# A graph attention kernel: when and where the gathers of source rows are issued

## The chip, the cores and the metric

The kernel runs on one core of a Trainium2 chip. The metric is device time in microseconds, the median of the runs shown. Five engines work side by side, each through its own list of instructions in order: PE (matmul), DVE (vector), ACT (scalar), POOL (GpSimd) and SP, which here only issues DMAs. They wait for one another by semaphores. POOL issues the indirect DMAs, which fetch table rows by a list of indices.

## The reference

One relational graph attention layer on 3125 nodes of 128 features and 100000 edges sorted by destination, with 5 edge types and 8 heads of 16 features, and two layer norms behind it. Cut to what matters:

```python
for r in range(R):
    q = einsum('eh,khd->ekd', x[dst], W_Q[r]); k = einsum('eh,khd->ekd', x[src], W_K[r])
    v = einsum('eh,khd->ekd', x[src], W_V[r])
    logits = (q * k).sum(-1) / 4 + attn_bias[r]            # only edges of type r
    e = exp(logits - segment_max(logits, dst)[dst])
    out += segment_sum(e / (segment_sum(e, dst)[dst] + 1e-12) * v, dst)
out = out.reshape(n, 128) @ out_proj_w.T + out_proj_b
h = layernorm(out + x) * ln_gamma + ln_beta
return layernorm(x + h)
```

## The kernel before

A first phase multiplies all nodes with all key and value weights and stores the rows in a table in HBM, `kv_d` (one row of 256 floats for each node and type), and the first queries in `q_d`. When the table is complete, the edges are worked through in 196 groups of 512 edges; a group is 4 tiles of 128 edges (`T = 4`).

The loop (L1062) counts steps `k`. In step k the logits of group k are made, and the values of an older group v are weighed with its softmax weights: weighing needs each destination node's maximum, and that needs the logits of all its edges. The distance is 16 to 18 steps at the start and 19 from group 22 on. All engines' orders are the order in which this loop emits instructions. What bears on the change:

- `gather(g)` (L678) fetches the key and value rows of group g into buffer `kvs_[g % KVB]`, 128 rows for each of 4 indirect DMAs, 1 KB a row, on POOL. The indices are columns of `idx`. A buffer may be written again when `weigh` (L878) of the group that was in it is done. There are `KVB = 22` buffers.
- `KVA = 9` groups are gathered ahead of the loop (L1059). In the loop, step k emits the gather of group k+2 (`AHEAD = 2`; k+1 in the last 16 steps), before the step's weighing (L1085).
- `logits(g)` (L756) multiplies the gathered keys with the spread queries on DVE and sums by head; `store_logits` (L764) writes them to `lg_d` from SP's queue.
- `maxima_load(b)` (L770) is an indirect DMA too, on POOL: it fetches for each of 128 nodes of block b the logits of its up to 64 edges (`ell`). It is emitted one step after the last group that may hold an edge of the block, behind this step's gathers. `maxima` (L779) works on it on ACT and DVE in the three following steps, 3, 4 and 5 of eight.
- The order on DVE within a step: `residual`, `weigh`, `less_max` of the next group to be weighed, `norm`, `logits`, `spot` (the 0/1 matrix `hot`, L735), the queries' remainders, `maxima`, `norms`. On PE: `spread_m`, `sums`, `spread_q`. On SP: the fetches of three steps ahead, stores of finished blocks, `fetch_m`, and the logits' store.

The lines of the loop that the change touches:

```python
        while gathered < NGR - 1 and step_of[gathered + 1] <= k + (AHEAD if k < final - 16 else 1):
            gathered += 1
            gather(gathered)
        for b in range(NM):
            if full_step[b] + 1 == k:
                maxima_load(b)
```

Of the kernel before, what the change touches and what calls it, by code (L numbers as in the profile page):

```python
# [10 lines left out]
I32 = mybir.dt.int32  # L11
# [6 lines left out]
P = 128  # L18
# [22 lines left out]
T = GE // P  # L41
NGR = -(-E // GE)
# [11 lines left out]
AHEAD = 2  # L54
# [5 lines left out]
SB = P * E // N // SR  # L60
SPAD = 5
QB = 3
KVB = 22
HELD = 21
KVA = 9


@with_exitstack
# [40 lines left out]
def full_at(n, more=0):  # L109

    last = E // N * n + slack(n) + more
    return -(-min(E, last) // GE) - 1 if n < N else NGR - 1


def block_of(g, ends=tuple(P * (b + 1) for b in range(NT))):

    return min(
        b for b, n in enumerate(ends)
        if n >= N or E // N * n - slack(n) >= min(E, (g + 1) * GE)
    )  # L120
# [9 lines left out]
NM = len(MB)  # L130


def windowed_path(
# [4 lines left out]
    nc = tc.nc  # L138
# [4 lines left out]
    kv_d = dram.tile([((NT - 1) * P + 64) * R, KVW], F32, name="kv_d")  # L143
# [6 lines left out]
    def keep(name, shape, dt=F32):  # L150
        return const.tile(shape, dt, name=name)

    idx = keep("idx", [P, T, NGR], I32)
# [19 lines left out]
    def buffers(those):  # L173
        for i in those:
            kvs_[i] = ctx.enter_context(tc.tile_pool(name=f"kvp{i}", bufs=1)).tile(
                [P, T, KVW], F32, name=f"kv{i}"
            )

    at_once = range(KVA)
    buffers(at_once)  # L180
# [184 lines left out]
    def fetch_keys(g):  # L365
        kt = ahead.tile([P, T, P], BF16, name="kt")
        nc.sync.dma_start(kt.rearrange("w t p -> w (t p)"), key_d[g].partition_broadcast(P))
        live["kt", g] = kt

    def fetch_q(g):  # L370
        qw = ahead.tile([P, 3, H], BF16, name="qw")
        f = window(g, first5, SPE)
        nc.sync.dma_start(qw.rearrange("w s h -> w (s h)"), q_d[bass.ds(f, P), :])
        live["qw", g] = qw
# [268 lines left out]
    rows, counted = {}, 0  # L643
# [29 lines left out]
    ps = ctx.enter_context(tc.tile_pool(name="ps", bufs=2, space=PSUM))  # L673
    buffers(i for i in range(KVB) if i not in at_once)
    hold = ctx.enter_context(tc.tile_pool(name="hold", bufs=HELD))
    flow = ctx.enter_context(tc.tile_pool(name="flow", bufs=2))
    late_flow = ctx.enter_context(tc.tile_pool(name="late_flow", bufs=2))
    def gather(g):  # L678
        kv = kvs_[g % KVB]
        for t in range(T):  # L680
            nc.gpsimd.indirect_dma_start(  # L681
                out=kv[:, t, :], out_offset=None, in_=kv_d[:, :],
                in_offset=bass.IndirectOffsetOnAxis(ap=idx[:, t, g : g + 1], axis=0),
            )


    def fetch_x(name, b):
# [68 lines left out]
    def logits(g):  # L756
        kv, lg = kvs_[g % KVB], live["lg", g]
        prod = flow.tile([P, T, H], F32, name="prod", bufs=1)
        nc.vector.tensor_tensor(prod, kv[:, :, :H], live.pop(("qe", g)), op=ALU.mult)  # L759
        nc.vector.tensor_reduce(  # L760
            lg[:, :, :HEADS], prod.rearrange("p t (k d) -> p t k d", d=HD), AX.X, ALU.add
        )

    def store_logits(g):  # L764
        nc.sync.dma_start(
            lg_d[g * GE : (g + 1) * GE, :].rearrange("(p t) c -> p (t c)", t=T),
            live["lg", g].rearrange("p t c -> p (t c)"),
        )

    def maxima_load(b):  # L770
        ell = late_flow.tile([P, D, LW], F32, name="ell", bufs=1)
        nc.gpsimd.indirect_dma_start(  # L772
            out=ell.rearrange("p s c -> p (s c)"), out_offset=None,
            in_=lg_d[: (full_at(MEND[b], D) + 1) * GE, :],
            in_offset=bass.IndirectOffsetOnAxis(ap=start_i[:, b : b + 1], axis=0),
        )
        live["ell", b] = ell
# [100 lines left out]
    def weigh(g):  # L878
        wv, kv = late_flow.tile([P, T, PW], F32, name="wv"), kvs_[g % KVB]
        live["wv", g] = wv  # L880
        nc.vector.tensor_tensor(  # L881
            wv[:, :, :H].rearrange("p t (k d) -> p t k d", d=HD),
            kv[:, :, H:].rearrange("p t (k d) -> p t k d", d=HD),
            live["mde", g][:, :, :, None].to_broadcast([P, T, HEADS, HD]),
            op=ALU.mult,
        )
# [60 lines left out]
    def by_node(g):  # L947
        f = window(g, first, ACTE)
        nc.scalar.copy(oT[:, bass.ds(f, WN)], live.pop(("op", g)))  # L949
# [63 lines left out]
    def store_z(b):  # L1013
        n = min(P, N - b * P)
        nc.sync.dma_start(out[b * P : b * P + n, :], live.pop(("z", b))[:n, :])


    step_of, n = {}, 0
# [4 lines left out]
    final = step_of[NGR - 1]  # L1023
# [5 lines left out]
    full_step = [step_of[full_at(n, D)] for n in MEND]  # L1029
# [3 lines left out]
    at_k, k = {}, 0  # L1033
    for v in range(NGR):
        k = max(k + 1, ready[block_of(v, MEND)])
# [21 lines left out]

    gathered = 0
    for gathered in range(KVA):  # L1059
        gather(gathered)  # L1060
    assert all(q_from[b] >= 2 for b in range(QB, NT))
    for k in range(-2, root_at[NT] + 2):  # L1062
        v, g = v_at.get(k), group_at.get(k)
        q_step = {k - f: b for b, f in enumerate(q_from) if b >= QB and -2 <= k - f <= 5}

        if k >= 0 and k + 3 in group_at:
            fetch_keys(group_at[k + 3])
            fetch_q(group_at[k + 3])
        if -2 in q_step:
            fetch_x("xq", q_step[-2])  # L1070
        for b in range(NT):
            if done_at[b] - 1 == k:
                fetch_x("xr", b)
            if norm_at[b + 1] + 1 == k:
                store_z(b)
        for b in range(NM):
            if ready[b] - 3 == k:
                store_m(b)
        if 5 in q_step:
            store_q(q_step[5])  # L1080
        for u in range(NGR):
            if max(at_k[u] - 3, ready[block_of(u, MEND)] - 2) == k:
                fetch_m(u)

        while gathered < NGR - 1 and step_of[gathered + 1] <= k + (AHEAD if k < final - 16 else 1):  # L1085
            gathered += 1
            gather(gathered)
        for b in range(NM):
            if full_step[b] + 1 == k:
                maxima_load(b)  # L1090

        for b in range(NT):
            if done_at[b] + 1 == k:
                residual(b)
        if v_at.get(k - 4) is not None:
            by_node(v_at[k - 4])
        if v_at.get(k - 2) is not None:
            carry(v_at[k - 2])
        if 1 in q_step:
            turned(q_step[1])  # L1100
        if 3 in q_step or 4 in q_step:
            second_part()
        if 2 in q_step or 3 in q_step:
            first_part()

        if v_at.get(k + 1) is not None:
            spread_m(v_at[k + 1], 8 if k + 1 in group_at else 12)
        if v_at.get(k - 1) is not None or v_at.get(k - 3) is not None:
            sums(v_at.get(k - 1), v_at.get(k - 3))
        if k + 1 in group_at:  # L1110
            spread_q(group_at[k + 1])

        if v is not None:
            weigh(v)
        if v_at.get(k + 1) is not None:
            less_max(v_at[k + 1])
            exps(v_at[k + 1])
        if v is not None:
            weights(v)
        if k + 1 in group_at:  # L1120
            types(group_at[k + 1])
        if v_at.get(k - 2) is not None:
            norm(v_at[k - 2])
        if g is not None:
            logits(g)
            store_logits(g)
        if k + 2 in group_at:
            spot(group_at[k + 2])
        if v_at.get(k + 1) is not None:
            places(v_at[k + 1], 2 if k >= final - 1 else 0)  # L1130
        if 3 in q_step or 4 in q_step:
            third_part()
        if 2 in q_step or 3 in q_step:
            remainder()
        for b in range(NM):
            whole = MB[b][2] is None
            if ready[b] - 6 == k and whole:
                maxima(b, 0, 2)
            if ready[b] - 5 == k and whole:
                maxima(b, 2, 4)  # L1140
            if ready[b] - 4 == k:
                maxima(b, 4 if whole else 0, R)
        for b in range(NT):
            if done_at[b] == k:
                project(b)
        for b in range(NT + 1):
            if root_at[b] == k:
                roots(b)
            if norm_at[b] == k:
                norms(b)  # L1150
        if 0 in q_step:
            turn_q(q_step[0])
        if 1 in q_step:
            queries(q_step[1], 0, RH)
        if 2 in q_step:
            queries(q_step[2], RH, R)
# [505 lines left out]
```

## Time and profile before

| | us |
|---|---|
| timed runs, median (range of 3) | 1240.98 (1237.96 to 1241.49) |
| profiled execution, its own time | 1596.71 |
| its span in the profile | 1594.9 |
| first gather issued, last one issued | 89.1, 1516.8 |
| busy: PE, DVE, ACT, POOL | 978.5, 931.1, 636.1, 797.2 |
| mean granted PE clock | 0.707 of full speed |

The profiled execution is longer than the timed runs by 356 us; durations of single instructions come from it. Some groups of instructions of the page's list, each with line, engine, operation, written and read tiles, count, busy time and mean ns of one, and the idle time of the engine just before them with what ended it:

```profile
L759 DVE TENSOR_TENSOR prod<-kv,qe 128x512 f32<-128x512 f32 x196 | 132.8, 678 | 83.2 <-remote 62.1
L881 DVE TENSOR_TENSOR wv<-kv,me 128x512 f32<-128x512 f32 x196 | 132.8, 677 | 42.1 <-remote 32.6
...
L772 POOL DMA_INDIRECT ell<-lg_d,start_i x25 | 23.6, 945 | 149.1 <-DMA lg_d<-lg 52.4
```

"remote" is a wait whose releaser the profile does not tell; "issue" is time in which the engine waited for nothing that the profile shows. [...]

### The profile page before, as it was taken

How to read it: one execution, taken by the hardware profiler on the slowest of the kernel's cores; microseconds unless marked ns; L12 is line 12 of the kernel's file. 1: busy time of each engine (PE TensorE's matmuls, PEld its weight loads, DVE VectorE, ACT ScalarE, POOL GpSimd, SP SyncE). 2: the span in 40 equal slices, each digit the busy share in tenths (PEclk: the TensorE clock that was granted, in tenths of full speed). 3: DMA queues.
4: the chain of work that ended last, by engine and by line, in shares of the span. 5: the costliest groups of instructions: out<-in, count | busy, mean ns of one | idle time of the engine just before them, and what ended most of it. 6: DMA issues, size and time to landing. Idle time of an engine off the chain costs nothing. (4 is left out here: it accounts for less than half of the span.)

```text
span 1594.9 us, 25686 instructions
## 1 busy us (share of the span) xinstructions
PE 978.5 (61%) x7526; PEld 752.9 (47%) x7526; DVE 931.1 (58%) x2559; ACT 636.1 (40%) x2248; POOL 797.2 (50%) x901
## 2 busy tenths in 40 slices
PE   7931423655676676667566657566676556565786
PEld 3520322434555554555454545455555444454664
DVE  5521623645756656656655656556665665664786
ACT  2620121324434444443453444343444344344454
POOL 3455446254555555555555555555555555455400
PEclk9965556766777767777776777676777777767678
DMA  6963634444545545555554554455555455444410
GB/s 191 357 195 97 153 85 128 103 109 122 139 120 128 144 121 121 138 131 122 119 132 105 133 136 121 117 133 123 129 138 133 111 138 134 111 127 119 102 27 15
DMA packets 180889, 203.63 MB, mean 128 GB/s; under 512 B 83207, under 2 KB 146083, under 8 KB 180620
## 3 DMA queue, kind: packets, MB, share of 16 engines
q0 software_dynamic: 40896, 113.39, 25.4%
q1 hardware_dynamic: 135414, 83.80, 23.4%
q10 hardware_dynamic: 4430, 4.71, 1.2%
q8 instruction: 63, 1.03, 0.3%
q14 instruction: 86, 0.70, 0.2%
HBM read 166.50 MB, written 35.28 MB: 127 GB/s over the span
## 5 line engine op out<-in xcount | busy, mean ns | idle before, releaser
L681 POOL DMA_INDIRECT kv<-kv_d,idx x784 | 742.5, 947 | 534.3 <-DVE den L936 252.9
L915 PE MATMUL pp<-wv,at 128*125 128x136 f32 x1568 | 399.6, 386 | 68.3 <-issue 62.1
L915 PEld LDWEIGHTS pp<-wv,at 128*125 128x125 f32 x1568 | 298.1, 256 | 154.8 <-issue 149.9
L746 PE MATMUL qe<-qw,hot 125*128 125x128 bf16 x2352 | 235.3, 261 | 139.9 <-issue 69.1
L863 PE MATMUL me<-mw,hot 125*128 125x64 bf16 (+1 forms) x2352 | 150.4, 217 | 237.5 <-issue 112.2
L746 PEld LDWEIGHTS <-hot 125*128 125x128 bf16 x2352 | 207.9, 127 | 158.4 <-issue 89.0
L872 DVE TENSOR_TENSOR me<-lg,me 128x32 f32<-128x32 f32 x196 | 37.8, 193 | 395.8 <-remote 247.0
L863 PEld LDWEIGHTS <-hot 125*128 125x128 bf16 x2352 | 130.9, 114 | 264.6 <-issue 232.9
L876 ACT ACTIVATE me<-me 128x32 f32<-128x32 f32 x196 | 35.7, 182 | 511.7 <-DVE me L872 318.6
L901 ACT ACTIVATE at<-row_at,nkey 128x125 f32<-128x125 f32 x744 | 237.5, 398 | 0.0
L759 DVE TENSOR_TENSOR prod<-kv,qe 128x512 f32<-128x512 f32 x196 | 132.8, 678 | 83.2 <-remote 62.1
L881 DVE TENSOR_TENSOR wv<-kv,me 128x512 f32<-128x512 f32 x196 | 132.8, 677 | 42.1 <-remote 32.6
L760 DVE TENSOR_REDUCE lg<-prod 128x32 f32<-128x512 f32 x196 | 134.4, 686 | 6.7
L904 ACT ACTIVATE at<-at 128x500 f32<-128x500 f32 (+1 forms) x196 | 117.4, 599 | 6.2
L917 PE MATMUL pp<-pt,carried 125*5 125x136 f32 x390 | 100.4, 346 | 30.7 <-issue 16.3
L707 PE MATMUL prq<-wq,xTq 128*128 128x384 f32 (+1 forms) x88 | 48.5, 639 | 81.0 <-DVE rem L717 59.9
L772 POOL DMA_INDIRECT ell<-lg_d,start_i x25 | 23.6, 945 | 149.1 <-DMA lg_d<-lg 52.4
L924 PEld LDWEIGHTS pp<-rsum,o 125*128 125x128 f32 x392 | 84.0, 258 | 18.7 <-issue 18.1
L949 ACT COPY oT<-pp 128x25 f32 x196 | 33.7, 172 | 135.9 <-remote 89.1
L810 DVE TENSOR_TENSOR wl<-by_head,shut 128x1024 f32<-128x1024 f32 (+2 forms) x73 | 76.9, 1053 | 17.2 <-issue 10.3
L924 PE MATMUL pp<-rsum,o 125*128 125x25 f32 x392 | 74.4, 270 | 18.3 <-issue 13.7
L816 DVE TENSOR_REDUCE mx<-wl 128x16 f32<-128x1024 f32 (+2 forms) x73 | 76.5, 1048 | 2.5
(184 smaller groups left out, 1018.6 us busy)
## 6 DMA issues: line engine op xcount, KB each, us to landing
kt<-key_d SPq DMA_DIRECT2D x196, 128.0 KB
qw<-q_d SPq DMA_DIRECT2D x196, 96.0 KB
kv_d<-kvs SPq DMA_DIRECT2D x24, 640.0 KB
kv<-kv_d,idx POOLq DMA_INDIRECT x784
q_d<-q SPq DMA_DIRECT2D x22, 480.0 KB
lg_d<-lg SPq DMA_DIRECT2D x196, 18.0 KB
mw<-m_d SPq DMA_DIRECT2D x196, 6.0 KB
xr<-in_x SPq DMA_DIRECT2D x24, 64.0 KB
```

Of the source, the lines that this page charges most:

```text
L681: nc.gpsimd.indirect_dma_start(out=kv[:, t, :], out_offset=None, in_=kv_d[:, :], in_offset=bass.IndirectOffsetOnAxis(ap=idx[:, t, g : g + ...
L746: nc.tensor.matmul(qe[:, t, :], hot[:, t, :], qw[:WR, s, :], start=(s == 0), stop=(s == 2))
L759: nc.vector.tensor_tensor(prod, kv[:, :, :H], live.pop(("qe", g)), op=ALU.mult)
L760: nc.vector.tensor_reduce(lg[:, :, :HEADS], prod.rearrange("p t (k d) -> p t k d", d=HD), AX.X, ALU.add)
L810: nc.vector.tensor_tensor(wl, by_head[:, None].to_broadcast([P, n, nh, D]), shut[:, :n, None, :].to_broadcast([P, n, nh, D]), op=ALU.add,)
L863: nc.tensor.matmul(me[:, t], hot[:, t, :], mw[:WR, None, :, s, :].to_broadcast([WR, times, 2, HEADS // 2]), start=(s == 0), stop=(s == 2),)
L881: nc.vector.tensor_tensor(wv[:, :, :H].rearrange("p t (k d) -> p t k d", d=HD), kv[:, :, H:].rearrange("p t (k d) -> p t k d", d=HD), live ...
L901: nc.scalar.activation(at[:, t, :], row_at[:, :WR], AF.Abs, bias=nkey[:, t, g : g + 1], scale=1.0)
L904: nc.scalar.activation(at[:, on_dve:], at[:, on_dve:], AF.Relu, bias=1.0, scale=-1.0)
L915: nc.tensor.matmul(pp, at[:, t, :], wv[:, t, :], start=(t == 0), stop=(t == T - 1))
L917: nc.tensor.matmul(pp[:R], carried[:WR, g, :], live.pop(("pt", g - 1)), start=False, stop=False,)
L924: nc.tensor.matmul(op, live.pop(("o5", done)), rsum[:WR], start=True, stop=True)
```

## The change

Gathers are issued in two halves. Ahead of the loop 6 groups are gathered instead of 9. In step k the first half (2 tiles) of group k+2 is emitted after this step's weighing. The second half takes its indices from a new small tile, `rows`, which DVE copies from `idx` after this step's logits. The maxima load moves behind the second half. The gathers stay two steps ahead to the end. There are 21 buffers instead of 22.

```diff
-KVB = 22
+KVB = 21
-KVA = 9
+KVA = 6
...
-    def gather(g):
+    def gather(g, t0, rows):
         kv = kvs_[g % KVB]
-        for t in range(T):
+        for t in range(T // 2):
             nc.gpsimd.indirect_dma_start(
-                out=kv[:, t, :], out_offset=None, in_=kv_d[:, :],
-                in_offset=bass.IndirectOffsetOnAxis(ap=idx[:, t, g : g + 1], axis=0),
-            )
+                out=kv[:, t0 + t, :], out_offset=None, in_=kv_d[:, :],
+                in_offset=bass.IndirectOffsetOnAxis(ap=rows(t), axis=0),
+            )
+
+    def first_gathers(g):
+        gather(g, 0, lambda t: idx[:, t, g : g + 1])
+
+    def more_gathers(g):
+        rows = flow.tile([P, T // 2], I32, name="rows", bufs=3)
+        nc.vector.tensor_copy(rows, idx[:, T // 2 :, g])
+        gather(g, T // 2, lambda t: rows[:, t : t + 1])
...
     for gathered in range(KVA):
-        gather(gathered)
+        first_gathers(gathered)
+        gather(gathered, T // 2, lambda t: idx[:, T // 2 + t, gathered : gathered + 1])
...
-        while gathered < NGR - 1 and step_of[gathered + 1] <= k + (AHEAD if k < final - 16 else 1):
-            gathered += 1
-            gather(gathered)
-        for b in range(NM):
-            if full_step[b] + 1 == k:
-                maxima_load(b)
...
         if v is not None:
             weigh(v)
+        ahead_of = []
+        while gathered < NGR - 1 and step_of[gathered + 1] <= k + AHEAD:
+            gathered += 1
+            ahead_of.append(gathered)
+            first_gathers(gathered)
...
         if g is not None:
             logits(g)
             store_logits(g)
+        for u in ahead_of:
+            more_gathers(u)
+        for b in range(NM):
+            if full_step[b] + 1 == k:
+                maxima_load(b)
```

## The prediction

> **What bounds the kernel now.** I read the page's slices first, then the gathers' own row, then the timeline of the loop's start, then a table of stretches, one for each step.
>
> ```profile
> DVE  5521623645756656656655656556665665664786
> ...
> POOL 3455446254555555555555555555555555455400
> ...
> L681 POOL DMA_INDIRECT kv<-kv_d,idx x784 | 742.5, 947 | 534.3 <-DVE den L936 252.9
> ```
>
> By the page no engine is full: DVE is at six tenths, POOL at five, and POOL idles 534 us before its gathers, half of it until the DVE instruction after a weighing. Read alone, this says that compute is late and gathers wait. The loop's start on DVE says why:
>
> ```profile
> 101.06 0.81 DVE L737 TENSOR_SCALAR hot<-kt,row_of 125x512 bf16<-125x512 bf16 x2 [0.64 <-DMA kv<-kv_d,idx]
> 122.19 0.69 DVE L759 TENSOR_TENSOR prod<-kv,qe 128x512 f32<-128x512 f32 x1 [20.31 <-issue]
> 122.91 0.69 DVE L760 TENSOR_REDUCE lg<-prod 128x32 f32<-128x512 f32 x1
> 123.52 0.34 DVE L737 TENSOR_SCALAR hot<-kt,row_of 125x512 bf16<-125x512 bf16 x1
> 154.32 0.69 DVE L759 TENSOR_TENSOR prod<-kv,qe 128x512 f32<-128x512 f32 x1 [30.46 <-remote]
> ```
>
> DVE stands still for 20 and 30 us, and no engine's work ends either wait. What covers both is POOL: it issues 48 gathers without a break from 89.1 to 149.0. In the loop it is the same in small. These are three neighbouring steps, each from one weighing to the next (columns: length, then busy time and instructions of each engine, PE clock, DMA share, GB/s):
>
> ```profile
> 826.80:837.70 10.90, 7.23 (x67) 5.84 (x68) 7.52 (x21) 6.73 (x17) 7.38 (x8) 0.84 0.72 160
> 837.70:851.60 13.90, 6.22 (x38) 4.39 (x38) 5.57 (x14) 2.56 (x11) 4.91 (x6) 0.54 0.34 82
> 851.60:857.50 5.90, 4.35 (x45) 3.31 (x42) 5.52 (x19) 2.77 (x11) 3.81 (x4) 0.92 0.46 96
> ```
>
> The second and third hold the same DVE work, 5.5 us; one takes 13.9 us, the other 5.9. In the long one POOL ends a run of 12 gathers (829.4 to 844.1), and DVE goes on at 846.7, after it. So in the profiled execution compute stands still while gathers run on back to back.
>
> **How that stands to the timed runs.** The profiled execution took 1596.7 us (span 1594.9 and 1.8 around it), the timed median is 1241.0: 356 us less. The standstills cannot be there in full. What must be there is POOL's own work. In a run of gathers one starts every 1.25 us (91.82, 93.08, 94.33). First gather at 89.1; 784 gathers x 1.25 = 980; 25 maxima loads on the same queue x 1.25 = 31; from the last gather's end (1516.8) to the end 78; outside 2. Sum 1180, which is 61 below the median. So I read the timed runs as held by POOL's queue nearly throughout, and each microsecond that POOL waits is a microsecond more. In the profiled frame the same sum leaves 417 us of standing still.
>
> **The change, part by part.**
>
> *Buffers 22 to 21, and the first two tiles after the weighing.* Weighing of group v is 19 steps after its logits (from the program's tables; 16 to 18 at the start). Before, gather g is free after weighing of g-22, which is in step g-3. Now it needs g-21, in step g-2: one step later. No instruction is added; a step of slack goes.
>
> *Two tiles behind the logits.* 190 groups (196-6) get one DVE copy of 128x2 integers. No such row exists; the nearest is `den`, 125x8, 159 ns by its row, 0.12 from its start to the next one's. Below zero is excluded, as it is new work. Lower end 0 (DVE waits for POOL anyway), upper 190 x 0.12 = 23 us; I take two exposed copies per block of eight steps. The wait is the real part: queued behind the waiting gather on POOL are the maxima load and the next group's gathers; for those wait the next logits.
>
> Against the copy speaks the Trainium skill, page "SBUF — State Buffer", section "Who interferes with whom": a DVE copy with source and destination in SBUF can take the port pair that GpSimd needs to write descriptors, and then blocks it for the whole instruction. The kernel already has such an operation, the `hot` comparison:
>
> ```profile
> L681 POOL DMA_INDIRECT kv<-kv_d,idx x784: 940/946/1209, 89.1 to 1515.8; - x196
> ...
> L737 DVE TENSOR_SCALAR hot<-kt,row_of x196: 335/344/579, 101.1 to 1512.3; 125x512 bf16<-125x512 bf16 x196
> ```
>
> (min/median/max ns.) By start times 113 of the 196 `hot` begin inside a gather, yet gathers keep 940 to 946 at minimum and median, where a block would add up to 340. By the rule the copies add up to 190 x 0.16 = 30 us; by the rows nothing. I take the rows.
>
> *What the loss of slack costs.* A block is eight steps (128 nodes). Steps 3, 4, 5 of it carry the maxima; their DVE work is 7.5, 5.6 and 5.5 us by the table, while POOL needs 5.0 a step. Put 0 at the end of POOL's issue of group 3. Its data land 1.7 us later (median, from the order of packets in the gather queue), and its logits (2 x 0.69) end at 3.2. POOL ends group 4 at 5.0 and the maxima load `ell`, next on the queue, at 6.25; that lands at 8.7 (2.45, same way). DVE reached it at 3.7 and waits. The rest of step 3 is 7.5 less 3.2 already done, and 0.4 for ACT's copy of `ell`: step 3 ends at 13.4.
>
> - Before: group 7 needs the weighing of step 4, over at 14.1; POOL gets to it at 6.25 + 10 = 16.25. Group 8 needs step 5's, over at 19.7; POOL is there at 21.25. No wait.
> - After: group 6 needs step 4's weighing. POOL is there at 11.25, starts at 14.4 (0.28 from a weighing's end to a gather's start, 803.56 to 803.84): 3.1 lost. Its second half finds the logits done, and ends at 19.4. Group 7 starts at 20.0: 0.6. Group 8: 0.5. With the two copies 4.4 us a block.
>
> 22 blocks have such a load and gathers after it: 22 x 4.4 = 97 us. That is the upper end. The lower: the 61 us over POOL's floor are waits for compute that are there already, 2.5 us for each of about 24 blocks; if they lie in the same heavy steps they count once: 22 x 1.9 = 42. The two ends rest on the same row; I take the middle, 69.
>
> *The maxima load moved* behind both halves and past `logits`: in this order of POOL's work it comes after group k+2 in both kernels, so by itself nothing; if the second half waits for logits, it is later by that wait, to 5 us a block at most, inside the sum above in part. Its old waits for the stored logits (52.4 us in 5 times by its row) belong to the standstills.
>
> *Six groups ahead.* POOL is through six groups at 119.0, through the next first half at 121.5, and then needs the logits of step 4. PE had the first product ready at 104.5, and bare steps took 2.2 us (logits at 163.0, 165.4, 167.6), so undisturbed these logits are done at about 115: nothing. If step 4 is as late as in the profile (161), 40 us at most.
>
> *Two steps ahead to the end* instead of one in the last 16: the order on POOL moves only against three maxima loads, between -3 and +3; I take 0. SP and ACT queues keep their order.
>
> Sum: 1241.0 + 69 = **1310**, own range 1283 to 1338. In the profiled execution the sign may be the other one: runs of eight and more gathers are broken by the waits, so its standstills should shrink; I expect a profiled span near 1400.
>
> **The rivals.**
>
> *Hidden anyway (chance 0.13).* If gathers go faster unprofiled than 1.25 us, or PE at half clock (the page's clock row alternates about 0.7) holds the loop, POOL has slack again and only exposed copies count: 0 to 23 us, 1250. For it: DVE and PE need 4.4 and 4.9 us a step in the profile, close to POOL's 5.2. Against: the floor alone explains 1180 of 1241.
>
> *Faster (0.22), 1200.* Timed runs hold part of the standstill behind back-to-back gathers, and the lockstep breaks these runs into twos. The place is the eight gathers of neighbouring groups, the price in the profile 8 us a time (13.9 against 5.9). It decides as soon as a block loses more by it than the lock's 4.4 us; at 6.3 us a block the gain is 22 x 1.9 = 41. For it: no other mechanism in the profile costs as much. Against: 61 us over the floor is all there is room for, unless the floor too is slower than in truth.
>
> *The lock is tighter (0.08), 1365.* `ell` comes late by the second half's wait in each block, 5 us more on some half of the blocks: +55 on 1310.
>
> *The change doesn't do what it says* is partly so: groups 6 to 20 have fresh buffers, so their first halves wait for no weighing; only the copy holds them. That is in the sums.
>
> **How the numbers follow.** Main case 0.57, hidden 0.13, tighter 0.08, faster 0.22. About 0.3% is what a measurement of this kernel can tell from no change, 1237 to 1245; of the hidden case 0.05 falls there. Slower: 0.57 + 0.08 + 0.08 = 0.73. The range must leave out at most 0.2: below, half of the faster case (down to 1215), above, most of the tight one (1345).
>
> **What would show it.** In the profile after: (1) POOL's idle time before gathers ends by the weighing and by the copy, and no run of more than some four to six gathers is left; (2) DVE waits for `ell` in step 3 grow; (3) gathers stay at 946 ns; (4) first logits near 105, not 122. If timed runs are faster, POOL was not their bound, and the step that fails is the floor.

## The result, and the profile after

The changed kernel takes 1333.78 us (median of 4 runs, 1331.93 to 1343.83), the kernel before 1241.24 (4 runs, 1237.96 to 1244.12): a ratio of 1.0763, with a 95% interval from 1.0702 to 1.0824. The forecast was 1310, own range 1283 to 1338. The profiled execution of the changed kernel took 1331.93, so here profile and runs agree. Here and below, ratios and intervals leave out runs that lie over 1.5% above the fastest of their kernel, so a ratio can differ a little from that of the two medians beside it.

One fact is needed to read all that follows. The kernels were measured in seven jobs, each on one chip and each with the kernel before beside the others. In some jobs the kernel before takes 1241 to 1249 us, in others 1582 to 1590, with the same program. I call them **quick** and **stalling** chips. Six of the jobs have their chip on record, six different ones (1 and 13 quick; 0, 4, 12 and 15 stalling). None of them was met twice, so a trait of the chip and something else that differs between jobs can't be told apart. Ratios are taken only within a job. The result above is of the quick kind; the profile of before that the prediction was read from took 1596.7, like the stalling chips.

The page of the changed kernel, the lines that answer to those of before (slices of the span in tenths, then the gathers: busy, mean ns, idle before them and what ended most of it):

```profile
DVE  4554557768777876876976876877787687687786
...
POOL 2637776666667667567656656766766766666300
...
L681 POOL DMA_INDIRECT kv<-kv_d,idx x404 | 383.8, 950 | 261.8 <-DVE den L945 142.8
L681 POOL DMA_INDIRECT kv<-kv_d,rows x380 | 363.8, 957 | 131.9 <-issue 76.6
```

POOL's first halves idle 143 us until a weighing is over (`den` stands two instructions behind one on DVE, and starts as the weighing ends). The loop's start on DVE, in the timeline of the changed kernel:

```profile
100.70 0.62 DVE L746 TENSOR_SCALAR hot<-kt,row_of 125x512 bf16<-125x512 bf16 x2 [1.00 <-DMA kv<-kv_d,idx]
102.80 0.69 DVE L768 TENSOR_TENSOR prod<-kv,qe 128x512 f32<-128x512 f32 x1 [1.48 <-issue]
103.52 0.69 DVE L769 TENSOR_REDUCE lg<-prod 128x32 f32<-128x512 f32 x1
```

No standstill of 20 us, although POOL issues gathers without a break beside it. And three steps of one block, from weighing to weighing (columns as in the prediction):

```profile
812.22:828.75 16.53, 7.74 (x73) 6.33 (x73) 7.42 (x22) 6.51 (x16) 9.48 (x10) 0.73 0.62 160
828.75:834.64 5.89, 4.73 (x38) 3.92 (x38) 5.72 (x14) 2.56 (x11) 3.79 (x4) 0.60 0.34 83
834.64:840.90 6.26, 3.38 (x38) 2.45 (x36) 5.88 (x19) 2.77 (x11) 3.79 (x4) 0.95 0.63 132
```

A later run of the kernel before on a quick chip (`before_look` below, 1243.4 us) gives the same three steps of the same block:

```profile
763.13:776.78 13.65, 8.59 (x73) 7.28 (x73) 7.59 (x22) 6.71 (x17) 8.92 (x11) 0.75 0.72 180
776.78:782.52 5.74, 4.12 (x34) 3.43 (x35) 5.57 (x13) 2.56 (x11) 4.51 (x5) 0.68 0.49 125
782.52:788.42 5.90, 5.18 (x43) 3.84 (x40) 5.52 (x19) 2.77 (x11) 3.82 (x5) 0.74 0.58 137
```

The first of them, step 3, is where most of the time goes: DVE's work is 7.4 against 7.6 us, the length 16.5 against 13.7. In the mean of 17 blocks (the 6th to the 22nd) step 3 is 2.8 us longer, the whole block of eight steps 4.2. All weighings from step 44 to 184 take 838 us in the changed kernel and 771 in the one before, 5.99 and 5.51 a step. What POOL does in that block shows in its timeline (start, length, idle before it and releaser):

```profile
816.24 0.95 POOL L681 DMA_INDIRECT kv<-kv_d,rows  x1 [0.30 <-issue]
817.49 0.95 POOL L681 DMA_INDIRECT kv<-kv_d,rows  x1 [0.30 <-issue]
818.75 0.95 POOL L781 DMA_INDIRECT ell<-lg_d,start_i  x1 [0.30 <-issue]
820.00 0.95 POOL L681 DMA_INDIRECT kv<-kv_d,idx  x1 [0.31 <-issue]
...
823.76 0.95 POOL L681 DMA_INDIRECT kv<-kv_d,rows  x1 [0.30 <-issue]
829.70 0.94 POOL L681 DMA_INDIRECT kv<-kv_d,idx  x1 [5.00 <-DVE den L945]
```

The maxima load is issued until 819.70. On DVE, in the same stretch:

```profile
818.72 0.35 DVE L746 TENSOR_SCALAR hot<-kt,row_of 125x512 bf16<-125x512 bf16 x1
823.78 0.33 DVE L804 SCALAR_TENSOR_TENSOR mine<-slot,deg,ell 128x64 f32<-128x64 f32 x1 [4.71 <-DMA ell<-lg_d,start_i]
...
828.75 0.68 DVE L890 TENSOR_TENSOR wv<-kv,me 128x512 f32<-128x512 f32 x1
829.35 0.19 DVE L881 TENSOR_TENSOR me<-lg,me 128x32 f32<-128x32 f32 x1
829.45 0.16 DVE L945 TENSOR_SCALAR den<-pp 125x8 f32<-125x8 f32 x1
```

This is the chain as forecast: DVE waits for the load's data, then does the maxima, then the weighing of step 4 (828.75), and only 0.25 us after `den` starts does POOL go on, having stood for 5.0 us. Two shorter waits follow in the block, 1.19 and 1.56. The next block has 4.50, 1.19 and 1.56. Step 3 is longer than before because the load comes later in it: it is issued 6.5 us behind the step's weighing (812.22 to 818.75), at the end of gathers without a break, and in the kernel before 3.5 us behind it (763.13 to 766.60).

### The profile page after: what moved, and what is told of

It is laid out like the page before. It is cut to its first block, busy times and chain, and to the rows that moved or that the text cites. A ratio compares the mean times of both kernels' runs of the same rounds, so it can differ in the third digit from the quotient of the medians.

```text
span 1330.1 us, 26045 instructions
## 1 busy us (share of the span) xinstructions
PE 873.1 (66%) x7526; PEld 685.6 (52%) x7526; DVE 958.6 (72%) x2749; ACT 633.8 (48%) x2248; POOL 802.4 (60%) x901
## 4 chain that ended last, share of the span: by engine, by line
DVE 34%; PE 21%; DMA 20%; issue 12%; POOL 7%; ACT 4%; SPq 2%; DVEq 0%; ACTq 0%; POOLq 0%
DMA ell<-lg_d,start_i 8%; POOL kv L681 7%; PE pp L924 6%; DVE wl L819 5%; DVE prod L768 4%; DMA mw<-m_d 4%; DVE wv L890 4%; PE pr L395 3%; DVE mx L825 3%; PE me L872 3%; DVE lg L769 3%; DVE hot L746 2%; PE qe L755 2%; ACT by_head L796 2%; DMA kv<-kv_d,rows 2%
## 5 line engine op out<-in xcount | busy, mean ns | idle before, releaser
L681 POOL DMA_INDIRECT kv<-kv_d,idx x404 | 383.8, 950 | 261.8 <-DVE den L945 142.8
L681 POOL DMA_INDIRECT kv<-kv_d,rows x380 | 363.8, 957 | 131.9 <-issue 76.6
L924 PE MATMUL pp<-wv,at 128*125 128x136 f32 x1568 | 357.6, 362 | 1.0 <-DVE o L948 1.0
L924 PEld LDWEIGHTS pp<-wv,at 128*125 128x125 f32 x1568 | 267.8, 236 | 66.1 <-issue 64.2
L755 PE MATMUL qe<-qw,hot 125*128 125x128 bf16 x2352 | 206.9, 251 | 40.9 <-DVE hot L746 36.5
L872 PE MATMUL me<-mw,hot 125*128 125x64 bf16 (+1 forms) x2352 | 125.7, 210 | 143.6 <-DMA mw<-m_d 69.5
L755 PEld LDWEIGHTS <-hot 125*128 125x128 bf16 x2352 | 194.0, 123 | 47.4 <-DVE hot L746 44.1
L872 PEld LDWEIGHTS <-hot 125*128 125x128 bf16 x2352 | 112.9, 109 | 176.4 <-DVE wv L890 77.1
L926 PE MATMUL pp<-pt,carried 125*5 125x136 f32 x390 | 96.0, 337 | 135.4 <-ACT pt L939 135.0
L926 PEld LDWEIGHTS pp<-pt,carried 125*5 125x5 f32 x390 | 18.2, 86 | 174.2 <-ACT pt L939 153.4
L796 ACT COPY by_head<-ell 128x512 f32<-128x512 f32 x24 | 25.7, 1071 | 139.9 <-DMA ell<-lg_d,start_i 139.9
L804 DVE SCALAR_TENSOR_TENSOR mine<-slot,deg,ell 128x64 f32<-128x64 f32 x25 | 8.4, 336 | 115.5 <-DMA ell<-lg_d,start_i 115.5
L746 DVE TENSOR_SCALAR hot<-kt,row_of 125x512 bf16<-125x512 bf16 x196 | 82.7, 422 | 1.5 <-DMA kv<-kv_d,idx 1.0
```

Source lines behind the costliest of these rows:

```text
L681: nc.gpsimd.indirect_dma_start(out=kv[:, t0 + t, :], out_offset=None, in_=kv_d[:, :], in_offset=bass.IndirectOffsetOnAxis(ap=rows(t), axis=0),
L746: nc.vector.tensor_scalar(hot, live.pop(("kt", g))[:WR], row_of[:WR], None, op0=ALU.is_equal)
L755: nc.tensor.matmul(qe[:, t, :], hot[:, t, :], qw[:WR, s, :], start=(s == 0), stop=(s == 2))
L872: nc.tensor.matmul(me[:, t], hot[:, t, :], mw[:WR, None, :, s, :].to_broadcast([WR, times, 2, HEADS // 2]), start=(s == 0), stop=(s == 2),)
L924: nc.tensor.matmul(pp, at[:, t, :], wv[:, t, :], start=(t == 0), stop=(t == T - 1))
L926: nc.tensor.matmul(pp[:R], carried[:WR, g, :], live.pop(("pt", g - 1)), start=False, stop=False,)
```

## The experiments

### On stalling chips: before_again, after_again

The kernels unchanged. The first asks whether standing still belongs to profiling; the second takes the changed kernel on such a chip.

> The kernel before, unchanged, profiled a second time. The changed kernel's profiled execution has a span like its timed runs (1330), the one of before was 356 us longer than its timed runs. If that standing still belongs to the order of this kernel's work (gathers far ahead), it comes again: span 1500 to 1600. If it was an accident of one execution, the span is 1235 to 1245 and the profile shows at last what the timed runs do: POOL busy nearly throughout, its idle time before gathers under 60 us in the loop.

Measured: 1586.99 us beside 1590.24, ratio 0.9954 (0.9925 to 0.9984). The runs of the repeated kernel lie between 1568 and 1600, none near 1241. So standing still is no effect of the profiler; it is in the timed runs of some jobs.

> The changed kernel, unchanged. In the last set of runs the kernel before took 1590 us, as its first profile does, while it took 1241 us where the result was measured: the same program on another chip. If before takes 1590 again here: theory (standing still behind back-to-back gathers exists only there, and the waits between halves shorten it) says about 1510 to 1540, near the kernel with the maxima load between the halves (1507). If before takes 1241: 1334, as in the result. Rival (the changed kernel does not stand still anywhere): 1330 in both cases.

Measured: 1511.9 beside 1585.7, ratio 0.9533 (0.9487 to 0.9579): here the change is **faster**, by 4.7%. The same program took 1333.78 on the quick chip. The two profiles differ at the loop's start; on the stalling chip DVE's timeline has

```profile
118.88 0.69 DVE L768 TENSOR_TENSOR prod<-kv,qe 128x512 f32<-128x512 f32 x1 [16.73 <-issue]
119.61 0.69 DVE L769 TENSOR_REDUCE lg<-prod 128x32 f32<-128x512 f32 x1
...
125.92 0.69 DVE L768 TENSOR_TENSOR prod<-kv,qe 128x512 f32<-128x512 f32 x1 [5.30 <-remote]
```

where the quick chip began at 102.80. From 230 us on DVE is busy 0.72 of the time in the first 5 us of a run of gathers (with less than 0.8 us between two), and 0.26 after that; on the quick chip, same program, 0.71 and 0.77. So on a stalling chip compute stands still once gathers have run on for some 5 us, and on a quick chip it doesn't, at the same 0.95 us a gather. The row with the most idle time on DVE shows it in the kernel before, first on a stalling chip, then on a quick one (`before_look`):

```profile
L872 DVE TENSOR_TENSOR me<-lg,me 128x32 f32<-128x32 f32 x196 | 37.8, 193 | 395.8 <-remote 247.0
L872 DVE TENSOR_TENSOR me<-lg,me 128x32 f32<-128x32 f32 x196 | 37.4, 191 | 90.9 <-PE me L863 87.9
```

Three obvious causes don't fit these two profiles. The gathered rows don't land later: by the order of packets 1.8 us behind the issue (median), on the quick chip 2.3. The packets that fetch instructions (queue q8 of the page) take no longer: 0.96 us in both (median). And PE's lower clock (0.707 against 0.786) makes PE's work 978.5 us instead of 861.0, 117 us more, not 353.

### On a stalling chip: whole_after_weigh, ell_between, three_tiles, before_pad

`whole_after_weigh` is the changed kernel without the copies: all four tiles right after the weighing, 21 buffers.

```diff
             first_gathers(gathered)
+            gather(gathered, T // 2, lambda t: idx[:, T // 2 + t, gathered : gathered + 1])
-            ahead_of.append(gathered)
```

> The changed kernel with all four tiles issued after the weighing: no halves, no copies; 21 buffers, 6 ahead, order of the weighing and of the maxima load kept. Theory (the buffer freed one step later is what costs): the second half rarely waited, so only the exposed copies go, 5 to 15 us: about 1322. Rival (copies, their wait and the port): back to about 1245.

Measured: 1596.05 beside 1590.24, ratio 1.01 (1.0073 to 1.0127). Without the halves nothing is gained. What gains on such chips is the second half with its wait for the copy behind the logits.

`ell_between` is the changed kernel with the maxima load between the halves.

```diff
             first_gathers(gathered)
+        for b in range(NM):
+            if full_step[b] + 1 == k:
+                maxima_load(b)
...
             more_gathers(u)
-        for b in range(NM):
-            if full_step[b] + 1 == k:
-                maxima_load(b)
```

> The changed kernel with the maxima load issued between the two halves (before the copy) instead of behind the second one. Theory (loss of slack, with the late maxima load in it): the load is issued 2.5 us earlier, so step 3 of each block ends 2.5 us earlier and POOL's wait in step 4 shrinks by the same: 22 x 2.5 = 55 us less than the changed kernel, about 1279. Rival (the copies and the wait for the logits are the cost): nothing, 1334.

Measured: 1507.12, ratio 0.9474 (0.9393 to 0.9555), beside 0.9533 for the change itself in another job: no difference that these runs can tell. POOL has slack on such a chip, so the load's place doesn't decide there, and the run says nothing of the quick ones.

`three_tiles` is the kernel before with one gather in four left out from group 22 on, 174 in all.

```diff
-        for t in range(T):
+        for t in range(T if g < KVB else T - 1):
```

> The kernel before, but from group 22 on only tiles 0 to 2 are gathered; tile 3 keeps old rows. That takes 174 of 784 gathers away, 174 x 1.25 = 217 us of POOL's queue, and leaves all other engines' work. Theory (POOL's queue holds the timed runs): the time falls until compute holds it, by 60 to 150 us, to 1090 to 1180. Rival (compute holds the timed runs, POOL has slack): 1235 to 1245.

Measured: 1368.91, ratio 0.8586 (0.8517 to 0.8655): 221 us less, 1.27 for each gather left out. A full queue of POOL would give about the same, 1.25; the next run tells the two apart. `before_pad` is the kernel before with one POOL memset of 0.22 us ahead of each group's gathers.

```diff
     def gather(g):
+        nc.gpsimd.memset(pad, 0.0)
```

> The kernel before with one more instruction on POOL ahead of each group's gathers, a memset of a 128x128 tile that nobody reads (its time p is read from the profile; I expect 0.2 to 0.5 us with its issue). All else as before. Where before takes 1241: theory (POOL's queue holds it) says 196 p more, less the 61 us over the floor at most that may hide it: for p = 0.4 between 20 and 78 us. Rival (compute holds it): no change within 5 us. Where before takes about 1590, gathers wait for compute, POOL has slack, and both say no change, unless the pause between groups shortens the standing still: then less by tens of us.

Measured: 1587.36 beside 1581.52, ratio 1.0014 (0.9978 to 1.005). 196 x 0.22 = 43 us more of POOL's time cost nothing, where a queue without slack would have shown 2.7%. Taken together: on a stalling chip the price goes with the gathers, their number or their bytes, and not with POOL's busy time. Neither run met a quick chip, so the slope of POOL's queue there was not measured this way.

### On quick chips: the kernel before, seen at last

> The kernel before once more, for a profile from this chip. If this chip takes about 1245 us for it, the profile shows for the first time what POOL did in the timed runs of the result. Theory A (POOL's queue is the bound there): POOL's idle time before gathers from 200 us on is small, under 60 us in all, the gaps between gathers are 0.30 us, and the span is that of the timed runs. Rival (another engine or the clock holds the kernel and the changed one loses elsewhere): POOL still idles 100 us or more before gathers and DVE or PE has the small gaps. If this chip takes about 1585: the profile repeats the standing still behind runs of gathers.

Measured: 1243.4 us (one run), span 1241.5, beside 1244.75. The page:

```profile
L681 POOL DMA_INDIRECT kv<-kv_d,idx x784 | 745.3, 951 | 271.6 <-issue 197.1
```

and its list of waits (engine and line, what it waited for: total, times, longest):

```profile
POOL kv L681 <- issue: 197.1, 645, 0.6
...
DVE mine L795 <- DMA ell<-lg_d,start_i: 56.9, 21, 6.9
...
POOL kv L681 <- DVE den L936: 31.4, 47, 1.2
```

645 gaps of 0.3 us are the queue's own rhythm. What POOL stands beyond 0.30 us, from the first gather (89.0) to the end of the last (1161.7), adds up to 58.7 us. This is theory A: the wait for weighings, 31.4 us with the 0.30 in it, is small, and POOL hardly rests. Of the 58.7 some 39 lie ahead of maxima loads (17 times) and 19 ahead of gathers. In the block shown above POOL's timeline of the kernel before reads

```profile
766.60 0.94 POOL L772 DMA_INDIRECT ell<-lg_d,start_i  x1 [1.99 <-issue]
...
777.84 0.95 POOL L681 DMA_INDIRECT kv<-kv_d,idx  x1 [0.30 <-DVE den L936]
...
783.47 0.94 POOL L681 DMA_INDIRECT kv<-kv_d,idx  x1 [0.92 <-DVE den L936]
...
789.37 0.94 POOL L681 DMA_INDIRECT kv<-kv_d,idx  x1 [1.19 <-DVE den L936]
```

Behind the weighing of step 4 (776.78), where the changed kernel stands 5.0 us, there is no wait here beyond the 0.30.

### On quick chips: buffers and copies apart

Four kernels fill a square: with and without the copies behind the logits, 21 and 22 buffers. The place of the maxima load, the 6 groups ahead and the end are those of the change in all four.

`halves_22`:

```diff
-KVB = 21
+KVB = 22
```

> The changed kernel with 22 buffers again: the halves, their places and the copies stay, only the slack of one step comes back. On a chip where the kernel before takes about 1241 us: theory A (POOL's queue is the bound, and the changed kernel loses 5.0, 1.2 and 1.6 us in each block where a first half waits for the weighing one step too early): those waits fall to near nothing, since POOL then needs the weighing of three steps back; 60 us or more come back of the 93, so 1245 to 1275. Rival B (the loss is the second half's wait for the copy behind the logits and the maxima load behind it): the buffer changes little, 1310 to 1335. On a chip where the kernel before takes about 1585: theory A has no say, as POOL has slack there; if what gains there is the pauses behind the logits, the gain stays, 1500 to 1525; if it is the pauses behind the weighing, which a spare buffer takes away, it goes back to 1560 to 1600.

`whole_21` is the edit of `whole_after_weigh`, `whole_22` that with 22 buffers.

> The same with 21 buffers: the wait for the weighing of the same step is back, still no copies. Where the kernel before takes about 1245: if the weighing alone binds as well as the copy alone does (my sum of the prediction, 4.4 us a block), ratio 1.04 to 1.07, 1295 to 1335. Rival (the wait for the weighing is worth only what the 22nd buffer gave back beside the copies, 17 us): 1255 to 1275. Where it takes about 1585: as measured before, 1580 to 1610.

> The changed kernel with 22 buffers and no copies: all four tiles of group k+2 are emitted after the weighing of step k; 6 groups ahead, the place of the maxima load and two steps to the end stay. Neither a weighing of the step before nor the logits of the step can hold POOL then. Where the kernel before takes about 1245: theory A (with 22 buffers the whole loss that is left is the copy behind the logits): ratio 0.99 to 1.015, so 1235 to 1265. Rival C (the six groups ahead, the moved maxima load or the end cost most of it): 1290 to 1325. Where it takes about 1585: with no pause at all, no gain, 1570 to 1610.

Measured, each beside before in its own job, with POOL's standing beyond 0.30 us between the first and the last gather, from the profile:

| | us | ratio (95%) | POOL stands, us |
|---|---|---|---|
| before (before_look) | 1243.4 | | 58.7 |
| whole_22: no copies, 22 buffers | 1249.54 | 1.0045 (1.0022 to 1.0068) | 59.3 |
| whole_21: no copies, 21 buffers | 1314.49 | 1.0576 (1.0493 to 1.0658) | 127.3 |
| halves_22: copies, 22 buffers | 1327.57 | 1.0627 (1.0602 to 1.0652) | 135.4 |
| the change: copies, 21 buffers | 1333.78 | 1.0763 (1.0702 to 1.0824) | 141.6 |

Either lock alone costs about six points, both together under eight. They don't add, since both hang on the same step. With 22 buffers the stalled instruction is the second half instead of the first, in POOL's timeline of `halves_22`:

```profile
824.34 0.95 POOL L681 DMA_INDIRECT kv<-kv_d,idx  x1 [0.30 <-issue]
828.98 0.95 POOL L681 DMA_INDIRECT kv<-kv_d,rows  x1 [3.69 <-DVE hot L746]
...
834.71 0.94 POOL L681 DMA_INDIRECT kv<-kv_d,rows  x1 [1.04 <-DVE hot L746]
...
840.65 0.94 POOL L681 DMA_INDIRECT kv<-kv_d,rows  x1 [1.25 <-DVE hot L746]
```

(`hot` is the instruction behind the copy.) In `whole_21` it is the whole gather, behind the weighing:

```profile
813.38 0.94 POOL L681 DMA_INDIRECT kv<-kv_d,idx  x1 [5.80 <-DVE den L945]
...
819.00 0.94 POOL L681 DMA_INDIRECT kv<-kv_d,idx  x1 [0.93 <-DVE den L945]
...
824.90 0.94 POOL L681 DMA_INDIRECT kv<-kv_d,idx  x1 [1.19 <-DVE den L945]
```

So my expectation for `halves_22` under theory A, 1245 to 1275, was a miss; its rival held, and what was wrong was to think of one lock where there are two. For `whole_22` and `whole_21` the expectations held. `whole_22` bounds the earlier gathers of the end, the 6 groups and the load's new place together: they cost 0.2 to 0.7%. That is for a load behind gathers that don't wait; behind a second half that waits for its copy, the load's place was not tested on a quick chip.

`before_21` is the kernel before with 21 buffers.

```diff
-KVB = 22
+KVB = 21
```

> The kernel before with 21 buffers and nothing else of the change. Where the kernel before takes about 1241 us: theory A: a whole gather waits for the weighing of the step before its own, emitted ahead of that step's weighing, so it runs one step tighter; by the block sum 3 to 5 us a block on 22 blocks, +66 to +110, so 1305 to 1350. Rival B: the buffer costs nothing by itself, 1241 to 1255. Where the kernel before takes about 1585: POOL has slack, so within 1% of it either way, 1570 to 1600, unless pauses behind the weighing shorten the standing still, then 1540 to 1570.

Measured: 1331.89 beside 1249.12, ratio 1.0659 (1.0633 to 1.0685). The number lies in theory A's range, but it is no test of it. In this kernel the gather of group k+2 stands ahead of the weighing in step k, which still needs the buffer; so from the weighing of group 22 on, where the distance is 19 steps, it works on the newer group's rows, and waits for them. The list of waits shows that it is DVE that waits:

```profile
DVE wv L881 <- DMA kv<-kv_d,idx: 161.8, 20, 11.0
```

It shows one thing all the same: with 21 buffers and two steps ahead, gathers can't stand where they stood before. The new place behind the weighing and the smaller count belong together.

### The load's lateness: ell_between_22

`halves_22` with the maxima load between the halves, the same edit as in `ell_between`.

> The changed kernel with 22 buffers and with the maxima load between the two halves of its step, one pair of gathers (2.5 us of POOL) earlier; copies stay. Beside it stands halves_22, which differs in the place of the load alone (1.0627 of before where before takes about 1245). In the changed kernel's profile the load is issued until 819.70 and its data are used at 823.78, 4.1 us later, where my prediction had 2.45; step 3 hangs on it, and POOL on step 4. Theory D: the whole lateness of the load passes on to POOL, so 2.5 us earlier gives 2.5 us in each of 22 blocks, 55 us: ratio 1.015 to 1.028, 1263 to 1281 where before takes about 1245; POOL waits 1.2 instead of 3.7 in the first place of the three. Rival E (DVE and PE work of steps 3 to 5 sets the waits, the load only happens to be late): 1.055 to 1.065. Where before takes about 1585: 22 buffers cost nothing of the gain there if it comes from the pauses behind the logits, 0.945 to 0.960.

Measured: 1531.3 beside 1589.36, ratio 0.965 (0.9608 to 0.9692), on a stalling chip, and a little above what was expected there. So theories D and E were not told apart: how much a load 2.5 us earlier gives back on a quick chip stays open. The gain of the halves with 22 buffers on stalling chips is there, 3.5%.

## Why the prediction was right

**The bound: right.** That the standstills of the profile were not in the timed runs was read from a floor of 1180 us, with 61 us left for waits of POOL. The profile of before on a quick chip has the first gather at 89.0, 79.8 from the last one's end to the end, and 58.7 of waits. The argument was sound, though its wording blamed the profiled execution; the same standstills are in the timed runs of four jobs.

**The lock: right in place, mis-sized by one term.** The three waits of 3.1, 0.6 and 0.5 are 5.00, 1.19 and 1.56 with the queue's 0.30 in each, so 4.70, 0.89 and 1.26 without it (the 3.1 still had the 0.30 in it, 2.85 without; the other two had not). The term is the landing of `ell`: put at 2.45 us behind the end of its issue, from the order of packets in the profile of before, it is used 4.1 us behind it in the block shown, and 3.9 in the median of 25 loads. Counted in the same way in the changed kernel's profile, it lands at 3.2, and its first use comes some 0.7 later, which the sum left out. These 1.65 us are most of the 1.85 missing in the first wait; the rest is the way from that use to the weighing, which took 4.97 us where 4.7 was worked out. The block loses 6.85 us instead of 4.4; 22 blocks would give 151, the profile has 141.6, as the first blocks lose less.

**Where I chose: the lower construction was the right one.** The lower end counted the 61 us of old waits once, the upper end not at all, and I took the middle, 69. Old waits do count once: the kernel before stands 39 us ahead of its maxima loads, the changed kernel before the last gather at none of them, as POOL is late already. With the right size, 151 - 61 = 90; measured are 1333.78 - 1241.24 = 92.5, and POOL's standing grows by 141.6 - 58.7 = 83. Of the rest, 5.5 us lie behind the last gather's end, 85.3 against 79.8; `whole_22` has 85.9 there too. That fits the two steps ahead to the end, which I put at nothing; it was not tested alone. That 1310 came as near as it did was partly luck: with the small size the lower construction gives 1283, with the right size the mean of both gives about 1360, and the two errors cancelled in part.

**Which wait binds: right only for 21 buffers.** The text had the second half find its logits done. With 21 buffers that is so; `halves_22` shows that a spare buffer brings out the copy's own lock, at nearly the same price. As a cause the lost buffer is worth 1.4 points of the 7.6 once the copies stand, and 5.3 without them (1.0576 against 1.0045).

**Copies and the shared port: right.** The Trainium skill, page "SBUF — State Buffer", section "Who interferes with whom", would have had the copies block descriptor writing, by my estimate 30 us in all. Gathers on `rows` have a median of 947 ns, before 946; the copies 158 ns. In the profile 150 of the 190 copies start inside a gather, and none of these gathers takes more than 956 ns. DVE may pay a little: `hot`, right behind a copy, has a mean of 422 ns against 365, hidden beside its waits; in `halves_22`, with the same copies, it has 359.

**Six groups ahead: right.** The first logits' product starts at 102.80 (I said about 105), before on a quick chip at 103.40.

**What it would show: (1) and the profiled span wrong.** Waits for weighings and for `ell` grew as said: DVE waits 115.5 us for `ell`, 4.8 a block where 5.0 was worked out, against 56.9 before. But runs of gathers did not break into four to six; from 793.5 to 824.7 POOL issues 24 and a load with no more than 0.31 us between two, since it is late there and finds every condition met. And the span is 1330, not 1400, as this chip doesn't stall; on one that does, it is 1511.8, shorter than before, as I said, but by far less than 1400 would be.

**The rival "faster"** named the right mechanism and the right condition, "timed runs hold part of the standstill". Where they do, the change gives 4.7%. On the quick chip they don't. So the forecast holds for the kind of chip whose timed runs it started from, and has the wrong sign for the other.

## What to carry to other kernels

When an in-order queue is the bound, ask of each wait put on it which step it hangs on, and look for the longest step of the period: a lock one step tighter costs nothing in five steps of eight, about 1 us in each of two, and 4.7 us in the one that stands behind a late load. Two locks that hang on the same step don't add, so undoing one tells little; build the square of both. If the profile's execution is far from the timed runs, work out what the timed runs can't do without, and run the same program again elsewhere before blaming either.

## What the runs showed of the hardware

The same kernel takes 1241 to 1249 us in three jobs and 1582 to 1590 in four, with the same 0.95 us a gather. On the stalling chips DVE falls from 0.72 to 0.26 busy after some 5 us of unbroken gathers, and much of its waiting has no releaser in the profile (247 of 396 us in the row above). Pauses behind the logits help there (0.9533 with 21 buffers); pauses behind the weighing alone don't (1.01), though 0.9474 with 21 buffers against 0.965 with 22, in two jobs, leaves them a smaller part. 43 us more of POOL's own time don't show (1.0014), each gather left out gives 1.27 us. Why some jobs stall was not found, nor whether it is the chip, and no kernel that was run on a quick chip beats the one before there; on the stalling ones the changed kernel (0.9533) and the ones with the load between the halves (0.9474, and 0.965 with 22 buffers) do.
